# A decoder layer on one core: one row of each q, k, v bias loaded first, and two tiles' projections held back

## The chip, the core and the metric

The kernel runs on one core of a Trainium2 chip. The core has five engines with a queue of instructions each: TensorE (PE, matrix products, with its weight loads shown apart as PEld), VectorE (DVE), ScalarE (ACT), GpSimd (POOL) and SyncE (SP), which issues the copies between the main memory and the core's memory. Every engine works through its queue in order and waits on semaphores for what others make. The time is device microseconds of one execution; smaller is better. The kernel before takes 1658.99 us (median of three runs, 1658.43 to 1659.1).

## The reference

Eight batches of 512 rows by 256 columns pass through three stages, each followed by a residual sum and a normalisation over the columns. All numbers are 32-bit floats. The first stage is the one that the change touches:

```python
xn = layer_norm(x, ln1_w, ln1_b)
q = (xn @ q_w.T + q_b).reshape(B, N, H, D).transpose(0, 2, 1, 3)
k = (xn @ k_w.T + k_b).reshape(B, N, H, D).transpose(0, 2, 1, 3)
v = (xn @ v_w.T + v_b).reshape(B, N, H, D).transpose(0, 2, 1, 3)
q = jax.nn.elu(q) + 1.0
k = jax.nn.elu(k) + 1.0
kv = jnp.einsum('bhnd,bhne->bnde', k, v)
qkv = jnp.einsum('bhnd,bnde->bhne', q, kv)
k_sum = k.sum(axis=1)
qk = jnp.einsum('bhnd,bnd->bhn', q, k_sum)
attn = qkv / qk[..., None]
attn = attn.transpose(0, 2, 1, 3).reshape(B, N, C)
attn = attn @ o_w.T + o_b
x = x + attn
xn2 = layer_norm(x, ln2_w, ln2_b)
h = jax.nn.gelu(xn2 @ fc_w.T + fc_b, approximate=False)
x = x + (h @ proj_w.T + proj_b)
```

The sums over heads (H = 16) are made for each row by itself, so no row needs another row of its batch. The second stage is softmax attention of 16 heads of 64 over a context of 512 rows; here all rows of the context count for every query. The third is an expert network: eight small encoder and decoder pairs are tried on a batch, the one with the least loss is chosen, and its adapter is applied.

## The kernel before, in words

A batch is four tiles of 128 rows, numbered 0 to 3; tile 2 is the third. For each tile the first stage runs as follows (the function `tile_attention`). PE multiplies the normalised, transposed tile `xnT` by the weights `wqkv`: 512 columns of q and k into one PSUM bank, 256 columns of v into another (L512 to L523). The bias is added in one of two ways. For tiles 0 and 1 of the first batch (`EARLY`, L64) PE adds a product of a row of ones with row 0 of `bqkv` (L519); for all others DVE adds the whole of `bqkv`, the same row copied to 128 partitions (L527, L544). ACT makes the exponential part (L531, L532, one buffer `ex`); DVE writes k and q (L554, L566). Then come eight large products over 1088 elements each, on POOL or on DVE, and eight sums on DVE: four for kv (L580, L589) and four for the output (L603, L612; for tiles 0 and 1 of the first batch the latter products are DVE's alone). A reciprocal, a product (L628), a transpose (L653) and a projection (L657) end the tile's attention; a norm and the tile's MLP follow (L737, L712, L717, and the norm L409). In the first batch the cross-attention's first half begins when tiles 0 and 1 are normalised and transposed (L799, then L818); its second half needs tiles 2 and 3.

There are two buffers each for q, k, v and kv, four for products, one for `ex`, one for the transposed tile `xnT`, one for the normalised rows `xhat`, and four PSUM banks beside the two of the attention scores. The next batch's norm takes `xhat` only after the MLP of the first batch's last tile has used it.

The order of the work on each engine is not written by hand. The kernel describes each step as a task with an engine (or a choice of two), an estimated duration, a due time, what it reads and writes, and the weights it needs. A planner (`play`, L161 to L220) then runs a clock: whenever an engine is free it takes, among the tasks that are ready, the one due first, and emits it. The clock is the planner's own; on the chip the engines keep the order but not these times. A task can be ready at the earliest when its weights have arrived by an estimate: `arrive` (L268) counts the bytes of the loads in their order at 185 bytes a nanosecond. A parameter `after` holds a task back until a time on the planner's clock.

`HOLD` (L65) names such times for tiles 2 and 3 of the first batch: their kv products (L596) start at 65000 and 75000 ns at the earliest. Their projections aren't held. Because the projections of tiles 0 and 1 need `wqkv` and `bqkv` by the estimate, and those of tiles 2 and 3 only `wqkv` (L521), the planner puts tile 2's projection ahead of tile 0's.

All loads are issued by SP at the start, in the order of the code: x in four copies, ln1w, ln1b, the three thirds of `wqkv` (L310), the three thirds of `bqkv` (L314, 128 rows of 1 KB, each from the same row in the main memory), woT, bo1 and so on to the context and the next batches' x. SP's queue is not planned by the clock for these. POOL adds bo1 to x for each tile (L376 in the profile, called at L641).

Of the kernel before, what the change touches and what calls it, by code (L numbers as in the profile page):

```python
# [18 lines left out]
P = 128  # L19
B, S, C = 8, 512, 256  # L20
# [41 lines left out]
AFTER = {6: (30, 84)}  # L62

EARLY = (0, 1)  # L64
HOLD = {(0, 2): 65000.0, (0, 3): 75000.0}  # L65


@with_exitstack
def decoder(ctx: ExitStack, tc: tile.TileContext, t: dict, out: bass.AP):
    nc = tc.nc  # L70
# [45 lines left out]
    def task(  # L116
        engine, took, due, emit, reads=(), writes=(), weights=(), kind=None, slack=0.0, holds=(), after=0.0, others=(),
        two=False,
    ):
        k = Task(engine, took, due, emit, kind, slack)  # L120
        k.two = two
        k.on.update((e, (n, wait)) for e, n, wait in others)
        k.at = max([after] + [eta[n] for n in weights])
        before = {}
        for key in reads:
            writers, readers = last.setdefault(key, ([], []))
            before.update((id(d), d) for d in writers)
            readers.append(k)
        for key in writes:
            writers, readers = last.get(key, ([], []))  # L130
            before.update((id(d), d) for d in (*writers, *readers))
            last[key] = ([k], [])
        before.pop(id(k), None)
        for d in before.values():
            d.next.append(k)
        k.unmet = len(before)
        k.vals = list({id(v): v for v in (*(v for v, _ in (*reads, *writes)), *holds)}.values())
        k.makes = [v for v in {id(v): v for v in (*(v for v, _ in writes), *holds)}.values() if v.room]
        for v in k.vals:
            v.left += 1  # L140
        if not k.unmet:
            for e in k.on:
                ready[e].append(k)
        return k
# [123 lines left out]
    def arrive(name, shape):  # L268

        n = 4  # L270
        for s in shape:
            n *= s
        eta["now"] += n / 185
        eta[name] = eta["now"]
# [31 lines left out]
    ln1w, ln1b = column("ln1w", KC), column("ln1b", KC)  # L306
    wqkv = const.tile([P, KC, 3 * C], F32, name="wqkv")
    bqkv = const.tile([P, 3 * C], F32, name="bqkv")
    for i, n in enumerate("qkv"):
        nc.sync.dma_start(  # L310
            out=wqkv[:, :, i * C : (i + 1) * C], in_=t[f"w{n}T"].rearrange("(c p) n -> p c n", p=P)
        )
    for i, n in enumerate("qkv"):
        nc.sync.dma_start(out=bqkv[:, i * C : (i + 1) * C], in_=t[f"b{n}"].partition_broadcast(P))  # L314
    arrive("wqkv", [P, KC, 3 * C])
    arrive("bqkv", [P, 3 * C])
    woT, bo1 = chunked("woT", C, C), row("bo1", C)
# [44 lines left out]
    def mm(cols, n):  # L362

        return n * {512: 858.0, 256: 432.0, 128: 222.0}[cols]
# [102 lines left out]
    def chunks(v, cs=range(NT)):  # L467
        return [(v, (kc, c)) for kc in range(KC) for c in cs]


    def linear_attention(b, begins, step):
# [22 lines left out]
        for c in range(NT):  # L494
            tile_attention(b, c, begins[c], step, x, xnT, y1)
            n2.stats(c, begins[c] + 15.6 * step)
            task(
                "pool", 728, begins[c] + 16 * step,
                lambda e, c=c: add(e, x.t[:, c, :], x.t[:, c, :], y1.t[:, c, :]),
                [(y1, c), (x, c)], [(x, c)], others=[("dve", 420, 4000)], two=True,  # L500
            )
        return y1, n2

    def tile_attention(b, c, due, step, x, xnT, y1):
        cols = slice(c * P, (c + 1) * P)
        qk, ps_v, ex = Val("bank"), Val("bank"), Val("ex")
        q, k, v = Val("q"), Val("k"), Val("v")


        early = b == 0 and c in EARLY  # L510

        def project(ps, lo, hi):  # L512
            for kc in range(KC):
                nc.tensor.matmul(  # L514
                    ps.t[:, : hi - lo], xnT.t[:, kc, cols], wqkv[:, kc, lo:hi], start=kc == 0,
                    stop=kc == KC - 1 and not early,
                )
            if early:
                nc.tensor.matmul(ps.t[:, : hi - lo], ones[0:1, :], bqkv[0:1, lo:hi], start=False, stop=True)  # L519

        needs = ("wqkv", "bqkv") if early else ("wqkv",)  # L521
        task("pe", mm(512, 2 + early), due, lambda: project(qk, 0, 2 * C), chunks(xnT, [c]), [(qk, 0)], needs, "full")
        task("pe", mm(256, 2 + early), due + 1, lambda: project(ps_v, 2 * C, 3 * C), chunks(xnT, [c]), [(ps_v, 0)], needs, "full", holds=[v])  # L523
        if not early:
            task(
                "dve", 690, due + 0.1 * step,
# [44 lines left out]
        kv, o = Val("sc" if early else "kv"), Val("o")  # L571

        def kv_of():
            return kv.t[:, 0, : E1 * D1].rearrange("p (e d) -> p e d", d=D1) if early else kv.t

        for i, s in enumerate(range(0, D1, DSPLIT)):
            pr = Val("prod")

            def kv_product(e, s=s, pr=pr):
                (nc.gpsimd if e == "pool" else nc.vector).tensor_tensor(  # L580
                    pr.t.rearrange("p (d e h) -> p d e h", d=DSPLIT, h=H1),
                    k.t[:, s : s + DSPLIT, :].unsqueeze(2).broadcast_to([P, DSPLIT, E1, H1]),
                    v.t.unsqueeze(1).broadcast_to([P, DSPLIT, E1, H1]),
                    ALU.mult,
                )

            def kv_sum(s=s, pr=pr):

                nc.vector.tensor_reduce(  # L589
                    kv_of()[:, :, s : s + DSPLIT].rearrange("p e d -> p d e"),  # L590
                    pr.t.rearrange("p (d e h) -> p d e h", d=DSPLIT, h=H1),
                    AX.X,
                    ALU.add,
                )

            task("pool", 2490, due + (1 + 1.2 * i) * step, kv_product, [(k, 0), (v, 0)], [(pr, 0)], holds=[kv], after=HOLD.get((b, c), 0.0),  # L596
                 others=[("dve", 1340, 500 if b == 0 else 5000)], two=True)
            task("dve", 1280, due + (2.2 + 1.2 * i) * step, kv_sum, [(pr, 0)], [(kv, s)])
        for i, s in enumerate(range(0, H1, DSPLIT)):
            pr = Val("prod")  # L600
# [623 lines left out]
```

## Time and profile before

| | us |
|---|---|
| median of three runs | 1658.99 |
| the profiled execution, its own time | 1659.94 |
| its span in the profile | 1658.1 |
| PE busy | 1561.0 |
| DVE busy | 1321.9 |
| PE busy in 0 to 40, 40 to 80, 80 to 120 | 22.82, 25.12, 26.50 |
| PE busy in 120 to 160 | 39.91 |
| mean granted clock of PE | 0.978 |

The span is the time from the first to the last instruction that the profile shows; some 1.8 us lie around it. "Busy" is the sum of the times in which an engine had an instruction in work. A line of the timeline gives the start, the duration, the engine, the line of the code, the operation with the tile it writes and the tiles it reads, their shapes and how many instructions are merged; in brackets stands how long the engine had been idle and what released it. A matmul of 32-bit floats is two records. L291 stands for every weight that a small helper loads, and L376 for every plain sum.

### The profile page before, as it was taken

Reading aid. Unit: us, or ns where it says so; the run is one execution under the profiler, and the core shown is the slowest. Engines: PE = TensorE matmul, PEld = TensorE weight load, DVE = VectorE, ACT = ScalarE, POOL = GpSimd, SP = SyncE. Lnnn points to the kernel's source line nnn. Section 1 sums busy time; section 2 is a strip of 40 time slices with the busy share of each in tenths; the row PEclk is TensorE's granted clock in tenths of the full one; section 3 lists DMA queues with packets and bytes.
Section 4 is the critical chain, followed back from the end, with each engine's and each line's share of the span. In section 5 each row is a group of like instructions: output and inputs, shape, how many; then the busy total and the mean of one; then the engine's idle time right before and its main releaser. Section 6 shows DMA issues by size and latency. Waiting matters only on the chain.

```text
span 1658.1 us, 23850 instructions
## 1 busy us (share of the span) xinstructions
PE 1561.0 (94%) x7736; PEld 919.3 (55%) x7736; DVE 1321.9 (80%) x2248; ACT 1055.4 (64%) x2318; POOL 1020.2 (62%) x821
## 2 busy tenths in 40 slices
PE   5579999999999999989999999999999999999995
PEld 3446666654665556645566555555554654654562
DVE  6887996798889898959968899788989756776554
ACT  2257776678656796657765686567666577556543
POOL 6376986786669586758747595656967331443222
PEclk8779999999999999999999999999999999999998
DMA  8000000022112211221122222242222332233300
GB/s 266 1 1 1 1 1 1 7 51 52 51 31 68 67 27 32 57 77 39 38 52 63 79 55 65 60 118 70 66 77 71 95 80 64 74 106 89 90 6 30
DMA packets 176651, 94.43 MB, mean 57 GB/s; under 512 B 19936, under 2 KB 174048, under 8 KB 176528
## 3 DMA queue, kind: packets, MB, share of 16 engines
q1 hardware_dynamic: 175760, 91.32, 20.6%
q0 software_dynamic: 768, 1.60, 0.4%
q8 instruction: 62, 1.02, 0.3%
q14 instruction: 61, 0.50, 0.1%
HBM read 16.30 MB, written 4.19 MB: 12 GB/s over the span
## 4 chain that ended last, share of the span: by engine, by line
PE 64%; DVE 17%; ACT 6%; SPq 5%; issue 4%; POOL 2%; DMA 2%; DVEq 0%; POOLq 0%; ACTq 0%
PE bank L954 10%; PE sc L872 10%; PE bank L970 5%; PE bank L687 5%; SPq L938 5%; PE bank L712 5%; PE bank L918 5%; PE bank L818 4%; DVE nmax L879 4%; PE bank L514 3%; DVE o L612 3%; PE bank L825 2%; ACT p L887 2%; PE bank L992 2%; DVE kv L589 2%
## 5 line engine op out<-in xcount | busy, mean ns | idle before, releaser
L887 ACT ACTIVATE p<-sc,nmax 128x512 f32<-128x512 f32 x512 | 348.5, 691 | 127.5 <-DVE nmax L879 115.8
L898 POOL TENSOR_SCALAR p<-p,rinv 128x512 f32<-128x512 f32 x300 | 209.3, 710 | 294.5 <-DVE rinv L892 275.9
L879 DVE TENSOR_REDUCE nmax<-sc 128x2 f32<-128x1024 f32 x256 | 305.3, 1212 | 69.6 <-PE sc L872 69.3
L580 POOL TENSOR_TENSOR prods<-k,v 128x1088 f32<-128x1088 f32 x115 | 288.9, 2533 | 72.8 <-DVE k L554 38.8
L603 POOL TENSOR_TENSOR prods<-q,kv 128x1088 f32<-128x1088 f32 x107 | 266.7, 2516 | 37.6 <-DVE kv L589 24.8
L872 PE MATMUL sc<-kT,qT 64*128 64x512 f32 x1024 | 267.8, 628 | 4.1 <-ACT kT L371 1.8
L589 DVE TENSOR_REDUCE kv<-prods 128x68 f32<-128x1088 f32 x120 | 152.3, 1272 | 17.8 <-POOL prods L580 17.5
L612 DVE TENSOR_REDUCE o<-prods 128x68 f32<-128x1088 f32 x128 | 161.3, 1270 | 4.6 <-POOL prods L603 4.5
L918 PEld LDWEIGHTS bank<-ident,p 128*128 128x128 f32 x944 | 106.4, 141 | 88.9 <-issue 48.6
L896 ACT ACTIVATE p<-p,rinv 128x512 f32<-128x512 f32 x212 | 143.8, 732 | 6.2 <-DVE rinv L892 6.2
L872 PEld LDWEIGHTS sc<-kT,qT 64*128 64x128 f32 x1024 | 88.1, 188 | 105.4 <-issue 79.2
L908 DVE STREAM_TRANSPOSE blk<-p 128x512 f32<-128x512 f32 x200 | 130.9, 687 | 17.0 <-POOL p L898 9.3
L918 PE MATMUL bank<-ident,p 128*128 128x128 f32 x944 | 134.6, 278 | 9.3 <-ACT qT L829 2.6
L954 PE MATMUL bank<-pT,v 128*64 128x256 f32 x1040 | 128.2, 389 | 5.7 <-DMA pT<-blk 2.7
L954 PE MATMUL bank<-prods,v 128*64 128x256 f32 x1008 | 124.4, 389 | 6.9 <-DMA prods<-prods 6.1
L818 PE MATMUL bank<-x1T,Wq 128*128 128x512 f32 (+1 forms) x288 | 124.7, 556 | 0.8 <-ACT x1T L371 0.5
L970 PE MATMUL bank<-Wo,oT 128*128 128x256 f32 x512 | 121.1, 381 | 0.0
L712 PE MATMUL bank<-projT,h 128*128 128x256 f32 x512 | 119.0, 383 | 1.3 <-ACT kT L371 0.7
L712 PEld LDWEIGHTS bank<-projT,h 128*128 128x128 f32 x512 | 94.9, 190 | 28.1 <-issue 8.3
L970 PEld LDWEIGHTS bank<-Wo,oT 128*128 128x128 f32 x512 | 94.9, 190 | 26.9 <-issue 14.6
L687 PE MATMUL bank<-xT,fcT 128*128 128x512 f32 x224 | 105.9, 600 | 2.2 <-DVE x L717 1.1
L1111 DVE SCALAR_TENSOR_TENSOR h<-bank,decb,xT 128x512 f32<-128x512 f32 x128 | 88.9, 740 | 21.7 <-PE bank L1101 20.7
(140 smaller groups left out, 2676.8 us busy)
## 6 DMA issues: line engine op xcount, KB each, us to landing
prods<-blk SPq DMA_DIRECT2D x480, 64.0 KB, 2.0
pT<-blk SPq DMA_DIRECT2D x320, 64.0 KB, 2.0
prods<-prods SPq DMA_DIRECT2D x176, 64.0 KB, 2.0
pT<-prods SPq DMA_DIRECT2D x128, 64.0 KB, 2.0
x<-in_x SPq DMA_DIRECT2D x7, 512.0 KB, 5.3
out<-x SPq DMA_DIRECT2D x7, 512.0 KB, 3.1
ctx<-in_ctxT SPq DMA_DIRECT2D x8, 256.0 KB, 3.0
fcT<-in_fcT SPq DMA_DIRECT2D x1, 1024.0 KB, 7.7
```

The source lines that it names most:

```text
L580: (nc.gpsimd if e == "pool" else nc.vector).tensor_tensor(pr.t.rearrange("p (d e h) -> p d e h", d=DSPLIT, h=H1), k.t[:, s : s + DSPLIT, : ...
L603: (nc.gpsimd if e == "pool" else nc.vector).tensor_tensor(pr.t.rearrange("p (h e d) -> p h e d", h=DSPLIT, d=D1), q.t[:, s : s + DSPLIT, : ...
L612: nc.vector.tensor_reduce(o.t[:, s : s + DSPLIT, :], pr.t.rearrange("p (h e d) -> p h e d", h=DSPLIT, d=D1), AX.X, ALU.add)
L712: nc.tensor.matmul(ps.t[:, :C], of(f, c), projT[:, f, :], start=f == fs[0], stop=f == fs[-1])
L818: nc.tensor.matmul(ps_q.t[:, :n], Wq[:, kc, cols], x1T.t[:, kc, rows], start=kc == 0, stop=kc == KC - 1)
L872: nc.tensor.matmul(ps.t[:, i, :], qT.t[rows, c * P : (c + 1) * P], kT.t[rows, :], start=True, stop=True)
L879: lambda: nc.vector.tensor_reduce(nmax.t, ps.t, AX.X, ALU.max, negate=True), [(ps, 0)], [(nmax, 0)],
L887: lambda i=i, p=p: nc.scalar.activation(p.t, ps.t[:, i, :], AF.Exp, bias=nmax.t[:, i : i + 1], accum_out=ssum.t[:, i : i + 1]),
L898: nc.gpsimd.tensor_scalar(p.t, p.t, rinv.t[:, i : i + 1], 1.0, ALU.mult, ALU.mult)
L918: nc.tensor.transpose(bank.t[:, m * P : (m + 1) * P], p.t[:, m * P : (m + 1) * P], ident)
L954: nc.tensor.matmul(to, v2.t[:, m, cols], of, start=m == 0, stop=m == NT - 1)
L970: nc.tensor.matmul(ps.t[:, :C], oT.t[:, c * P : (c + 1) * P], Wo[:, pr, :], start=pr == prs[0], stop=pr == prs[-1])
```

## The change

Three edits, all for the first batch. First, each third of the bias is loaded in two copies: row 0 right after the third of the weights that it belongs to, and rows 1 to 127 after all three. Second, in the planner the projections of tiles 0 and 1 no longer need `bqkv`'s estimated arrival, only that of `wqkv`. Third, the time in `HOLD` now holds the two projections of tiles 2 and 3 (both matmul tasks), with 68000 and 78000 ns in place of 65000 and 75000; their products are no longer held by themselves.

```diff
-HOLD = {(0, 2): 65000.0, (0, 3): 75000.0}
+HOLD = {(0, 2): 68000.0, (0, 3): 78000.0}
...
     for i, n in enumerate("qkv"):
         nc.sync.dma_start(
             out=wqkv[:, :, i * C : (i + 1) * C], in_=t[f"w{n}T"].rearrange("(c p) n -> p c n", p=P)
         )
+        nc.sync.dma_start(out=bqkv[0:1, i * C : (i + 1) * C], in_=t[f"b{n}"].partition_broadcast(1))
     for i, n in enumerate("qkv"):
-        nc.sync.dma_start(out=bqkv[:, i * C : (i + 1) * C], in_=t[f"b{n}"].partition_broadcast(P))
+        nc.sync.dma_start(out=bqkv[1:P, i * C : (i + 1) * C], in_=t[f"b{n}"].partition_broadcast(P - 1))
     arrive("wqkv", [P, KC, 3 * C])
     arrive("bqkv", [P, 3 * C])
...
-        needs = ("wqkv", "bqkv") if early else ("wqkv",)
-        task("pe", mm(512, 2 + early), due, lambda: project(qk, 0, 2 * C), chunks(xnT, [c]), [(qk, 0)], needs, "full")
-        task("pe", mm(256, 2 + early), due + 1, lambda: project(ps_v, 2 * C, 3 * C), chunks(xnT, [c]), [(ps_v, 0)], needs, "full", holds=[v])
+        needs, begin = ("wqkv",), HOLD.get((b, c), 0.0)
+        task("pe", mm(512, 2 + early), due, lambda: project(qk, 0, 2 * C), chunks(xnT, [c]), [(qk, 0)], needs, "full", after=begin)
+        task("pe", mm(256, 2 + early), due + 1, lambda: project(ps_v, 2 * C, 3 * C), chunks(xnT, [c]), [(ps_v, 0)], needs, "full", holds=[v], after=begin)
...
-            task("pool", 2490, due + (1 + 1.2 * i) * step, kv_product, [(k, 0), (v, 0)], [(pr, 0)], holds=[kv], after=HOLD.get((b, c), 0.0),
+            task("pool", 2490, due + (1 + 1.2 * i) * step, kv_product, [(k, 0), (v, 0)], [(pr, 0)], holds=[kv],
                  others=[("dve", 1340, 500 if b == 0 else 5000)], two=True)
```

## The prediction

> **What bounds the kernel now.** I read the busy table first, then the busy time by stretches, then the timeline of the first 100 us, then the DMA view of the first 40 us.
>
> ```profile
> PE 1561.0 (94%) x7736; PEld 919.3 (55%) x7736; DVE 1321.9 (80%) x2248; ACT 1055.4 (64%) x2318; POOL 1020.2 (62%) x821
> ...
> 70.00:80.00 10.00, 7.27 (x48) 6.24 (x46) 8.99 (x5) 2.29 (x8) 9.50 (x5) 1.00 0.00 1
> 80.00:90.00 10.00, 1.04 (x3) 0.65 (x4) 9.97 (x13) 0.37 (x1) 8.28 (x4) 0.63 0.00 0
> ...
> 120.00:160.00 40.00, 39.91 (x231) 27.44 (x228) 29.03 (x58) 28.14 (x61) 20.41 (x24) 1.00 0.00 1
> 160.00:200.00 40.00, 37.21 (x225) 25.38 (x223) 38.74 (x55) 28.37 (x65) 36.26 (x19) 1.00 0.01 1
> 200.00:240.00 40.00, 39.77 (x238) 25.75 (x237) 38.27 (x55) 29.15 (x67) 38.66 (x22) 1.00 0.00 1
> ```
>
> The columns after a stretch and its length are PE, PEld, DVE, ACT, POOL, the granted clock and DMA. PE sets the time (94%), but it is full only from about 115 us; in 80 to 90 it works 1.04 us of 10 while DVE works 9.97. In 160 to 240 DVE is full too (77.0 of 80). So a gain or a loss comes from the first 90 us, and DVE has no room to make good after 160.
>
> ```profile
> 10.76 6.36 PE L514 MATMUL bank<-wqkv,xnT 128*128 128x512 f32 x12 [0.47 <-ACT xnT L461]
> ...
> 14.87 2.78 POOL L376 TENSOR_TENSOR y<-x,bo 128x256 f32<-128x256 f32 x4 [7.21 <-DMA bo<-in_bo]
> ...
> 20.56 8.42 POOL L580 TENSOR_TENSOR prods<-k,v 128x1088 f32<-128x1088 f32 x3 [2.91 <-ACT v L536]
> ...
> 30.22 0.58 DVE L554 SCALAR_TENSOR_TENSOR k<-bank,ex 128x256 f32<-128x256 f32 x1
> ...
> 34.26 2.04 PE L834 MATMUL bank<-ctx,Wk 128*128 128x512 f32 x2 [8.05 <-DMA ctx<-in_ctxT]
> ...
> 70.24 7.53 POOL L580 TENSOR_TENSOR prods<-k,v 128x1088 f32<-128x1088 f32 x3
> ...
> 80.04 0.40 DVE L717 TENSOR_TENSOR x<-x,bank 128x256 f32<-128x256 f32 x1
> ...
> 88.49 0.69 PE L799 MATMUL bank<-ident,x 128*128 128x128 f32 x2 [10.63 <-DVE x L409]
> ...
> 89.64 2.07 PE L818 MATMUL bank<-x1T,Wq 128*128 128x256 f32 x4 [0.46 <-ACT x1T L371]
> ```
>
> Each matmul is two records. The first 8 of the 12 at 10.76 are tile 2 (the third), then comes tile 0; the bank, k, q and v that tile 2 fills then lie idle until 70.24. Tile 1's k is written only at 30.22. POOL's adds at 14.87 wait for bo1, and stand in its queue ahead of the products. The cross-attention's first matmul is the one at 89.64; before it PE waits 10.63 us, because tile 1's last steps (L717, the norm, L409) stand in DVE's queue between tile 2's products and sums.
>
> ```profile
> DMA packets 9536, 11.03 MB, mean 276 GB/s; under 512 B 1600, under 2 KB 8256, under 8 KB 9536
> ...
> q1 hardware_dynamic: 9536, 11.03, 88.3%
> ...
> bqkv<-in_bq SPq DMA_DIRECT2D x1, 128.0 KB, 3.8
> ...
> wqkv<-in_wvT SPq DMA_DIRECT2D x1, 256.0 KB, 4.0
> ```
>
> The DMA engines are 88.3% busy in the first 40 us: 0.883 x 16 x 40 / 9536 = 59 ns a packet of 1157 B on average, so some 52 ns for 1 KB.
>
> **The change, part by part.**
>
> *Order at the start.* Tile 0's projection loses tile 2's 8 records ahead of it. PE starts at 10.76 as before, slow at first (weight loads 0.86 apart): 4 x 0.86 + 1.1 for the bias = 15.3; Relu 0.60, Exp 0.63, k 0.59: 17.1. v: 1.1 + 0.6 on PE, copy 0.60: 17.6. Products could start at 17.6, not 20.5: 2.9 earlier. Tile 1's k, q and v get the second buffers at once (about 22, not 30.2).
>
> *The bias copies.* Three 128-row copies become three of one row (1 KB each) and three of 127 rows. SP issues 3 more at 0.45: 1.35 for all that is queued behind them, and 0.47 and 0.9 for wk and wv. Wv issued at 4.52 and landed at 8.5; 9.4 is still ahead of 10.76, so that costs nothing (if PE were ready at once, 0.9). The single rows (nearest: the 1 KB ln1w, 2.3 us) are there long before the bias matmul at 14. No row shows a 127-row copy. One end: it is cut like the 128-row one, and costs what that costs. Other end: one engine takes all of it, since 127 is prime and 16 equal shares cannot be made: 381 packets x 52 ns = 20 us on that engine, against 1.2 on 16, and whatever is queued behind needs that engine too. I take the second end, because every copy on this queue in the trace has a row count that 16 divides and this one has none but 1.
>
> The Trainium skill speaks against this edit: "DMA: Bandwidth & Descriptors", section "Why a DMA increments its semaphore by 16 and not by 1", says that the number of engines must divide the outermost count, and names 127 partitions as a case of one engine. At its 27 GiB/s an engine the 381 KB take, as an estimate, 13.5 us and not 20, and the sum below would be 6.5 less, 1658.
>
> *Who waits for it.* Serial copies start when wv has landed, 8.5, and end at 28.5; woT and bo1 follow, 29.5. On POOL the planner puts bias-bo1 adds ahead of the products: by its arrival sums bo1 comes at 13.3 of its clock (9.1 for wqkv, then 2.1, 1.4, 0.7), tile 0's k is ready at 14.1 (9.1, matmuls 2.6, Relu, Exp and k 1.9, hops 0.5). Two adds of 0.7 come first, so POOL's first product runs at 30.9, 10.3 later than 20.56. DVE makes two of tile 0's four products meanwhile; POOL's other two (2.45 each) end at 35.8, the last sum (1.2) at 37.0, against 30.3. From there DVE owes 8 products and 8 sums (16 x 1.2), 4 sums of tile 1 (4.8) and tile 0's small steps (2): 26, so tile 1's last sum ends at 63, against 56.9. The rest of the weight queue goes 13 to 14 later, so ctx lands at 48, not 34.3; PE's L834 and L825 stand ahead of tile 0's transposes, which move from 46.3 to 54 (cover for this: none, tile 0 is ready at 50).
>
> *Tiles 2 and 3 wait with their projections.* PE's 2.6 us each (4 x 0.43 + 4 x 0.22), DVE's adds 0.70 and 0.60, ACT's 1.23, DVE's k and q 1.0 move behind tile 1's MLP: no instruction is added. Gain: tile 1's tail is free of tile 2. L712 ended at 77.9, L717 began at 80.0 (2.2 late), and from L717's end to L409's end went 8.0, where stats 0.6, 0.15, power 0.55, L409 0.5 and hops 0.3 make 2.1: 8.1 in all. So 63 + (32.7 - 8.1) = 87.6, and tile 0's later MLP in front on PE adds up to 3: cross-attention starts at 88 to 91, where it did. Loss: tile 2's products go from 70.2 to about 92 (its projection 5 us after L712). Of DVE's 19.0 us in 70 to 90, about 5.5 belong to tiles 0 and 1; 13.4 move past the start of the cross-attention. DVE's idle time from there to 160 is 0.7 + 4.0 + 4.2 + 6.8 = 15.6; it stands there for PE and ACT, so I let half be used, 7.8. Left over: 5.6, which nothing takes up in 160 to 240, and for which PE stands. Ends: all absorbed 0, none 13.4.
>
> **Sum.** The profiled run took 1659.94 (span 1658.1 and 1.8 around it), 0.95 above the median of 1658.99. 1659.94 + 5.6 = 1665.5; less 0.95, 1664.6 on the runs' scale: **1665**. All absorbed 1659, none 1672; 3 more where the start slips to 91, 1675.
>
> **Rivals.**
>
> *The copies spread (other side).* Then bo1 lands at 14.87 + 1.35 = 16.2, and POOL's products start at 17.6. Tile 1's last sum: 56.9 - 2.9 - 1.2 (tile 3's adds, gone from DVE's queue) = 52.8. Its transposes no longer wait behind tile 0's MLP (58.3 to 62.7, 4.4): cross-attention at 52.8 + 32.7 - 8.1 - 4.4 = 73 at best. Tile 2's work is then 8 us late instead of 22, so at most the hole of 10.6 counts; DVE's limit after 160 takes some 2: 1659 - 9 = **1650**. For it: the 128-row copy at 3.8 us. Against it: 127. It decides if bo1 lands before 20.5.
>
> *The stall is swallowed.* The copies are serial, but DVE uses all its 15.6 idle us before 160: **1659**. For it: 29.0 of 40 in 120 to 160. Against it: that idle time follows PE and ACT, and tile 3 comes last of the chain that opens batch 1 (one xhat buffer).
>
> *Batch 1 starts late.* Tile 3's MLP gates batch 1's norm; if none of the 13.4 is made good and the start slips too, **1675**. For it: DVE full in 160 to 240.
>
> *The edit does nothing.* If the bias matmul still waited for the 127-row copies, only the hold would act. Under serial copies that adds 13 us of wait at 15 and is worse than the forecast, so it sits in the upper end.
>
> **How the numbers follow.** Forecast 0.44 (its own range 1662.5 to 1670), late batch 1 0.12, swallowed 0.15, spread 0.29. 0.2% (3.3 us) is about what a measurement here can tell from no change. Slower: 0.44 + 0.12 = 0.56; within: 0.15; faster: 0.29. The range goes from the spread case to the late one, 1649 to 1676. A new plan also reorders everything that follows; I put no price on it beyond this range.
>
> **What would show it.** Right: bo1's landing and POOL's first add near 29, POOL's first product near 31, ctx at PE near 48, tile 2's products after 85, PE's wait before L799 shorter than 3, DVE fuller in 120 to 160. Wrong: POOL's adds at 16 (then the first rival); or DVE still at 29 of 40 in 120 to 160 with no loss of PE after 160.

## The result, and the profile after

The changed kernel takes 1668.06 us (median of five runs, 1667.08 to 1672.94); the kernel before, on the same chip, 1658.43 (1656.45 to 1659.10). The ratio is 1.0060, 95% interval 1.0044 to 1.0076: slower by 9.6 us of medians. The profiled execution took 1667.56 us, its span is 1665.8. Line numbers grow by two (L514 is now L516, L580 is L582, L799 is L801, L818 is L820).

The busy table and the busy time by stretches of the kernel after (columns: stretch, length, then PE, PEld, DVE, ACT, POOL, granted clock and DMA):

```profile
PE 1557.0 (93%) x7736; PEld 917.7 (55%) x7736; DVE 1318.5 (79%) x2256; ACT 1052.3 (63%) x2314; POOL 1017.4 (61%) x813
...
70.00:80.00 10.00, 8.52 (x56) 7.40 (x55) 5.49 (x20) 3.09 (x10) 3.53 (x5) 1.00 0.00 0
80.00:90.00 10.00, 8.12 (x34) 5.23 (x35) 3.87 (x10) 2.78 (x4) 1.91 (x3) 1.00 0.00 1
...
120.00:160.00 40.00, 36.15 (x216) 25.88 (x215) 30.88 (x57) 28.58 (x66) 25.30 (x24) 0.96 0.00 1
160.00:200.00 40.00, 37.74 (x211) 25.32 (x210) 36.54 (x47) 23.95 (x55) 32.84 (x15) 1.00 0.00 1
200.00:240.00 40.00, 36.48 (x212) 23.93 (x210) 38.80 (x65) 28.77 (x66) 34.82 (x20) 1.00 0.00 1
```

In 80 to 90 the picture is turned over: PE works 8.12 of 10 (1.04 before) and DVE 3.87 (9.97 before). The hole in front of the cross-attention is gone. The bill comes later: PE loses 3.85, 2.26 and 3.52 us in the last three stretches, 9.6 in all, where it lost 3.1. From 0 to 280 us PE idles 59.8 us in place of 49.1.

The timeline of the kernel after, with the lines that answer to those shown of before, in the same order:

```profile
10.49 3.03 PE L516 MATMUL bank<-wqkv,xnT 128*128 128x512 f32 x4 [0.47 <-ACT xnT L463]
...
27.34 1.40 POOL L378 TENSOR_TENSOR y<-x,bo 128x256 f32<-128x256 f32 x2 [19.95 <-DMA bo<-in_bo]
28.70 8.33 POOL L582 TENSOR_TENSOR prods<-k,v 128x1088 f32<-128x1088 f32 x3
...
21.86 0.58 DVE L556 SCALAR_TENSOR_TENSOR k<-bank,ex 128x256 f32<-128x256 f32 x1
...
46.14 2.04 PE L836 MATMUL bank<-ctx,Wk 128*128 128x512 f32 x2 [25.24 <-DMA ctx<-in_ctxT]
...
89.38 8.40 POOL L582 TENSOR_TENSOR prods<-k,v 128x1088 f32<-128x1088 f32 x3 [2.58 <-DVE k L556]
...
83.06 0.42 DVE L719 TENSOR_TENSOR x<-x,bank 128x256 f32<-128x256 f32 x1 [3.81 <-PE bank L714]
...
85.55 0.44 PE L801 MATMUL bank<-ident,x 128*128 128x128 f32 x2
86.91 1.13 PE L820 MATMUL bank<-x1T,Wq 128*128 128x256 f32 x4 [0.92 <-DVE x1T L375]
```

Tile 0 is first on PE, and tile 1's k is written at 21.86, 8 us earlier than before. But POOL stands 19.95 us for bo1, and its first product comes at 28.70 in place of 20.56, although k and v were ready by 16.9. The context reaches PE at 46.14 in place of 34.26. Tile 1's tail is as short as it can be: from L719's start at 83.06 to the transpose at 85.55 are 2.5 us, where L717's start and L799 were 8.45 apart. Tile 2's first product on POOL comes at 89.38 in place of 70.24.

SyncE's queue of the kernel after shows why bo1 is late, and the DMA view of its first 40 us what the engines did meanwhile (each digit and number is one microsecond). First two issues of the kernel before, then the kernel after:

```profile
6.02 0.43 SPq L314 DMA_DIRECT2D bqkv<-in_bv  x1
6.49 0.43 SPq L291 DMA_DIRECT2D woT<-in_woT  x1
```

```profile
6.04 0.25 SPq L316 DMA_DIRECT2D bqkv<-in_bq  x1
6.33 1.85 SPq L316 DMA_DIRECT2D bqkv<-in_bk  x1
8.22 5.71 SPq L316 DMA_DIRECT2D bqkv<-in_bv  x1
13.97 5.75 SPq L291 DMA_DIRECT2D woT<-in_woT  x1
19.77 0.60 SPq L291 DMA_DIRECT2D bo<-in_bo  x1
```

```profile
DMA  0187388500000000000048459999999999999999
GB/s 0 46 249 230 52 260 280 203 26 23 23 23 23 22 23 23 23 23 22 23 78 301 70 178 400 333 334 359 352 310 294 381 393 426 398 393 364 353 345 366
...
q1 hardware_dynamic: 6410, 8.02, 61.2%
```

From 8 to 20 us the core's DMA engines move 22 to 26 GB/s, against up to 280 just before and mostly over 300 later. The busy share of the queue in the first 40 us falls from 88.3% to 61.2%. In 8 to 20 us the 16 engines together are busy for 0.07 of their time (0.97 before), about one engine's worth: the 127-row copies run at the pace of a single engine, 1 KB in some 45 ns, and the issues behind them (in_bv, woT) take 5.7 us each in place of 0.4.

### The profile page after: what moved, and what is told of

Its sections match the earlier page's. It is cut to its first block, busy times and chain, and to the rows that moved or that the text cites. A ratio compares the mean times of both kernels' runs of the same rounds, so it can differ in the third digit from the quotient of the medians.

```text
span 1665.8 us, 23845 instructions
## 1 busy us (share of the span) xinstructions
PE 1557.0 (93%) x7736; PEld 917.7 (55%) x7736; DVE 1318.5 (79%) x2256; ACT 1052.3 (63%) x2314; POOL 1017.4 (61%) x813
## 4 chain that ended last, share of the span: by engine, by line
PE 61%; DVE 17%; SPq 7%; ACT 6%; issue 4%; DMA 3%; POOL 3%; DVEq 0%; POOLq 0%; ACTq 0%
PE bank L956 10%; PE sc L874 9%; PE bank L714 6%; SPq L940 5%; PE bank L689 5%; PE bank L972 5%; PE bank L920 4%; DVE nmax L881 4%; PE bank L820 3%; PE bank L516 3%; PE bank L827 3%; DVE o L614 3%; PE bank L994 2%; ACT p L889 2%; DVE kv L591 2%
## 5 line engine op out<-in xcount | busy, mean ns | idle before, releaser
L900 POOL TENSOR_SCALAR p<-p,rinv 128x512 f32<-128x512 f32 x291 | 204.3, 714 | 274.0 <-DVE rinv L894 247.6
L582 POOL TENSOR_TENSOR prods<-k,v 128x1088 f32<-128x1088 f32 x113 | 285.1, 2544 | 79.3 <-DVE k L556 42.6
L605 POOL TENSOR_TENSOR prods<-q,kv 128x1088 f32<-128x1088 f32 x110 | 272.5, 2499 | 45.2 <-DVE kv L591 27.0
L898 ACT ACTIVATE p<-p,rinv 128x512 f32<-128x512 f32 x221 | 150.7, 732 | 7.3 <-DVE rinv L894 7.3
L874 PEld LDWEIGHTS sc<-kT,qT 64*128 64x128 f32 x1024 | 86.9, 186 | 102.3 <-issue 73.8
L820 PE MATMUL bank<-x1T,Wq 128*128 128x512 f32 (+1 forms) x288 | 123.7, 552 | 1.5 <-DVE x1T L375 0.9
L972 PEld LDWEIGHTS bank<-Wo,oT 128*128 128x128 f32 x512 | 95.9, 192 | 27.0 <-issue 13.4
```

The lines of the kernel that those rows point to most:

```text
L582: (nc.gpsimd if e == "pool" else nc.vector).tensor_tensor(pr.t.rearrange("p (d e h) -> p d e h", d=DSPLIT, h=H1), k.t[:, s : s + DSPLIT, : ...
L605: (nc.gpsimd if e == "pool" else nc.vector).tensor_tensor(pr.t.rearrange("p (h e d) -> p h e d", h=DSPLIT, d=D1), q.t[:, s : s + DSPLIT, : ...
L874: nc.tensor.matmul(ps.t[:, i, :], qT.t[rows, c * P : (c + 1) * P], kT.t[rows, :], start=True, stop=True)
L900: nc.gpsimd.tensor_scalar(p.t, p.t, rinv.t[:, i : i + 1], 1.0, ALU.mult, ALU.mult)
L972: nc.tensor.matmul(ps.t[:, :C], oT.t[:, c * P : (c + 1) * P], Wo[:, pr, :], start=pr == prs[0], stop=pr == prs[-1])
```

## The experiments

The kernel before ran beside each on the same chip; its medians lay between 1657.1 and 1659.3. So times are compared by the ratio, and "us more" is the ratio less one, times 1658. "Rows" are those of the later copies of the bias, "first product" is tile 2's first on POOL, "MLP 3" is the first matmul of tile 3's MLP, the last step of batch 0 before batch 1 can begin; "PE idle" is 0 to 280 us. "Mark" is a point of the work near 500 us: the start of the 64th of DVE's 256 row maxima of the softmax (L879, at 498.97 in the kernel before), less its time before. "Order" is that of the instructions on DVE, POOL and ACT after this mark: the profiles show two, a and b, which differ nearly to the end of the kernel. These six columns are from the profiled executions, one of each kernel.

| kernel | rows | projections of tiles 2, 3 | cross-attention | first product | MLP 3 | PE idle | mark | order | ratio (95%) | us more |
|---|---|---|---|---|---|---|---|---|---|---|
| before | 128 | free, tile 2 first; products 65, 75 | 89.6 | 70.2 | 140.2 | 49.1 | 0 | a | 1 | 0 |
| after | 127 | held 68, 78 | 86.9 | 89.4 | 150.9 | 59.8 | 9.6 | a | 1.0060 (1.0044 to 1.0076) | 9.9 |
| e1 | 112 | held 68, 78 | 81.4 | 83.9 | 145.4 | 53.0 | 4.8 | a | 1.0049 (1.0035 to 1.0064) | 8.1 |
| e2 | 126 | held 68, 78 | 80.9 | 83.4 | 144.9 | 53.2 | 4.2 | a | 1.0033 (1.0020 to 1.0047) | 5.5 |
| e3 | 127 | as before | 102.1 | 82.7 | 152.4 | 55.4 | 12.2 | a | 1.0069 (1.0054 to 1.0085) | 11.4 |
| e4 | 128 | held 68, 78 | 80.8 | 82.7 | 145.6 | 44.2 | 2.6 | b | 1.0032 (1.0021 to 1.0043) | 5.3 |
| e5 | 127, late | held 68, 78 | 80.7 | 83.1 | 144.6 | 52.7 | 4.0 | a | 1.0048 (1.0035 to 1.0061) | 8.0 |
| e6 | 112 | free; products 65, 75 | 84.5 | 72.4 | 136.0 | 47.2 | -3.4 | a | 0.9997 (0.9987 to 1.0007) | -0.5 |
| e7 | 112 | held 48, 58 | 93.3 | 66.7 | 142.0 | 52.9 | 2.3 | b | 1.0061 (1.0047 to 1.0074) | 10.1 |
| e8 | 112 | held 40, 50 | 91.1 | 69.0 | 139.6 | 56.7 | 7.9 | b | 1.0085 (1.0072 to 1.0098) | 14.1 |
| e9 | 112 | tile 2 free, products 65; tile 3 held 78 | 84.8 | 73.5 | 135.7 | 48.0 | -3.1 | b | 1.0004 (0.9994 to 1.0015) | 0.7 |
| e10 | 112 | free; products 72, 82 | 82.0 | 78.0 | 139.8 | 50.0 | 2.3 | b | 1.0029 (1.0016 to 1.0043) | 4.8 |
| e11 | 128 | free; products 65, 75 | 84.3 | 72.1 | 135.7 | 46.9 | -3.4 | a | 0.9995 (0.9984 to 1.0005) | -0.8 |
| e12 | 112 | free; products 58, 68 | 92.8 | 65.5 | 140.3 | 49.0 | 0.7 | b | 1.0041 (1.0026 to 1.0056) | 6.8 |

PE's idle time of e4 can't be set beside the others: its first matmuls are longer (18.90 us busy for 29 records in 8 to 30; before 16.55 for 40), and PE's busy time is 1571.2 in all, 10 more than before.

The mark shows what a run lost or gained in its first 500 us. Two profiles of kernels with the same order (e6 and e11) agree in it to 0.1 us, while their spans end 5 us apart (1650.4 and 1655.4). From the mark to the end of the span, against the kernel before, the other kernels with order a change by -4.3 to 1.2 us, those with order b by 2.4 to 3.8. So some of what e4, e7 to e10 and e12 lose lies behind 500 us, where the planner put the work in another order; no run took this by itself. The prediction put no price on it; the kernel after has order a, as before, so its own loss holds none of it.

### Which copies are slow

**e1**: the single row becomes 16 rows, the rest 112.

```diff
-  out=bqkv[0:1, ...], in_=t[f"b{n}"].partition_broadcast(1)
+  out=bqkv[0:16, ...], in_=t[f"b{n}"].partition_broadcast(16)
...
-  out=bqkv[1:P, ...], in_=t[f"b{n}"].partition_broadcast(P - 1)
+  out=bqkv[16:P, ...], in_=t[f"b{n}"].partition_broadcast(P - 16)
```

> The changed kernel with its bias copies cut at row 16 in place of row 1: three copies of 16 rows, three of 112; order on all engines as in the changed kernel. Theory (the 127-row copies run on one engine and hold up all that is queued behind them): bo1 reaches POOL near 16 us in place of 27.3, POOL's first product near 17.5 in place of 28.7, ctx reaches PE before 37 in place of 46.1, cross-attention begins at 73 to 79 in place of 86.9, time 1650 (1645 to 1656). Rival (the loss is in the hold of tiles 2 and 3, not in the copies): the start moves, but the time stays over 1663.

**e2**: the rest is cut into 126 rows and one.

```diff
-  out=bqkv[1:P, ...], in_=t[f"b{n}"].partition_broadcast(P - 1)
+  out=bqkv[1 : P - 1, ...], in_=t[f"b{n}"].partition_broadcast(P - 2)
+  out=bqkv[P - 1 : P, ...], in_=t[f"b{n}"].partition_broadcast(1)
```

> The changed kernel with each 127-row copy cut once more: 126 rows and 1 row, so nine small or large copies in all. If what counts is a common divisor with the 16 engines (126 = 14 x 9), bo1 reaches POOL near 17 us and the time is within 4 us of the cut at row 16. If any row count that 16 does not divide is served by one engine, or if copies that begin at row 1 are slow, bo1 still comes near 28 and the time stays at 1664 to 1672.

**e5**: the 127-row copies stay, but SyncE issues them in the course of batch 0.

```diff
-    for i, n in enumerate("qkv"):
-        nc.sync.dma_start(out=bqkv[1:P, ...], in_=t[f"b{n}"].partition_broadcast(P - 1))
...
+        def rest():
+            for i, n in enumerate("qkv"):
+                nc.sync.dma_start(out=bqkv[1:P, ...], in_=t[f"b{n}"].partition_broadcast(P - 1))
+
+        task("sp", 0, 0.0, rest, after=45000.0)
```

> As the kernel after, but the three 127-row copies are issued by SP in the course of the first batch (at 45 us of the planner's clock), behind all the first loads, instead of ahead of woT and bo1. Theory (the copies cost only by what is queued behind them): bo1 at POOL before 16, ctx at PE before 37, cross-attention from 80 to 83, as with copies of 112 rows: 1664 to 1667. Rival (a 127-row copy costs wherever it runs, since it holds SP's queue and one engine): 1668 or more, with later loads (the next batch's x, the weights of stage two) late by some 15.

In all three the order of the work on DVE, ACT and POOL is that of the kernel after. SyncE's queue of e2:

```profile
6.41 0.26 SPq L317 DMA_DIRECT2D bqkv<-in_bq  x1
6.71 0.32 SPq L316 DMA_DIRECT2D bqkv<-in_bk  x1
7.07 0.26 SPq L317 DMA_DIRECT2D bqkv<-in_bk  x1
8.03 0.32 SPq L316 DMA_DIRECT2D bqkv<-in_bv  x1
```

One row fewer in the copy, and the 5.71 us are 0.32: bo1 reaches POOL at 14.0, the context PE at 35.2. So it is the count of 127, as the prediction took it, and neither the number of copies nor that they begin at row 1. In e5 the same slow copies run from 29.9 on (issues of 1.51 and 6.26 us, again mostly 22 to 24 GB/s) and nothing waits for them: the context is at PE at 32.8. A slow copy costs by what is queued behind it.

But all three are still slower than before, by 5.5 to 8.1 us. With the copies mended the cross-attention starts 8 to 9 us earlier than before the change, and the kernel loses more than half of the 9.9 all the same. The prediction's first rival (copies spread: 1650) is refuted, and with it the theory of e1; e1's rival held. The other half of the change costs by itself.

### The copies without the hold, and the hold without the copies

**e3**: before, with only the copies cut into 1 and 127 rows.

```diff
+  out=bqkv[0:1, ...], in_=t[f"b{n}"].partition_broadcast(1)
...
-  out=bqkv[:, ...], in_=t[f"b{n}"].partition_broadcast(P)
+  out=bqkv[1:P, ...], in_=t[f"b{n}"].partition_broadcast(P - 1)
```

> The kernel before, its order on all engines unchanged, with only the bias copies of the change (1 and 127 rows). Theory: bo1 reaches POOL near 27 us, its four adds end at 30, the first product starts near 30 in place of 20.6, ctx comes near 46, cross-attention begins at 95 to 99 in place of 89.6, time 1666 (1662 to 1672). Rival (the copies are hidden behind work that waits anyway): within 3 us of 1658.4.

**e4**: before, with only the hold moved from the products to the projections (128-row copies, and tiles 0 and 1 wait for the bias's estimate as before).

```diff
-HOLD = {(0, 2): 65000.0, (0, 3): 75000.0}
+HOLD = {(0, 2): 68000.0, (0, 3): 78000.0}
...
-  task("pe", mm(512, 2 + early), due, ..., needs, "full")
+  task("pe", mm(512, 2 + early), due, ..., needs, "full", after=HOLD.get((b, c), 0.0))
...
-  kv_product, ..., holds=[kv], after=HOLD.get((b, c), 0.0),
+  kv_product, ..., holds=[kv],
```

The second matmul task, for v, is held in the same way.

> The kernel before with only the hold moved from the products of tiles 2 and 3 to their projections (68000 and 78000 ns), bias copies of 128 rows and the planner's need for the bias as before. Theory: tile 0 comes first on PE all the same, because nothing else is ready; POOL's products begin at 17.5 to 18.5 us, cross-attention at 74 to 80, time 1651 (1646 to 1657). Rival (holding the projections pushes tiles 2 and 3 and so batch 1 back): 1663 or more.

The copies alone cost 11.4 us: the context is at PE at 46.8, tile 2's work stands in tile 1's way as before, the wait of PE for tile 1's norm remains, and the cross-attention starts at 102. PE of e3:

```profile
100.93 0.69 PE L800 MATMUL bank<-ident,x 128*128 128x128 f32 x2 [10.64 <-DVE x L410]
```

The hold alone costs 5.3 (2.6 of it by the mark, the rest in order b), where the theory of e4 had a gain of 7; its rival held. Together they cost 9.9, so the two do not add up. Where the copies are slow, the hold costs nothing that can be told (e3 and after, whose intervals overlap; after has the new order of tile 0 besides, and no run has that order and the slow copies without the hold); where they are fast, it costs 8.6 (e1 less e6, each by its ratio to before on its own chip; e2 in the place of e1 gives 6.0, e5 8.5, and at the mark the three give 7.4 to 8.2). Either half alone loses more than half of the 9.9.

### What in the hold costs

**e6**: fast copies, tiles 0 and 1 first, but the products are held as in the kernel before and the projections are free. Against e1:

```diff
-HOLD = {(0, 2): 68000.0, (0, 3): 78000.0}
+HOLD = {(0, 2): 65000.0, (0, 3): 75000.0}
...
-        needs, begin = ("wqkv",), HOLD.get((b, c), 0.0)
+        needs, begin = ("wqkv",), 0.0
...
-  kv_product, ..., holds=[kv],
+  kv_product, ..., holds=[kv], after=HOLD.get((b, c), 0.0),
```

> Copies of 16 and 112 rows and tiles 0 and 1 first, but no hold on the projections of tiles 2 and 3: their products are held, at 65 and 75 us of the planner's clock, as in the kernel before. Theory (the hold of the projections is what costs in the runs with fast copies): tile 2's products near 70, PE's idle time in 120 to 280 back to 4 to 6 us, 1656 to 1660. Rival (tile 0's earlier start with three products on DVE costs): 1663 to 1667 as with the hold.

Theory held: no difference from before that the measurement can tell. PE's idle time in 120 to 280 is 4.8 us, with the projections held (e1) it was 12.5. Where the 8.6 us come from is seen in the busy time of DVE and POOL ahead of the cross-attention. The stretch 58 to 81 of e1:

```profile
58.00:81.00 23.00, 20.35 (x108) 16.97 (x106) 9.13 (x31) 5.72 (x19) 4.49 (x7) 0.91 0.00 1
```

and of e6:

```profile
58.00:81.00 23.00, 15.35 (x94) 13.04 (x93) 15.35 (x30) 8.50 (x22) 9.48 (x7) 0.95 0.00 0
```

PE does 5 us more there in e1, but DVE (third pair) does 6.2 less and POOL 5.0 less: the kv products and sums of tile 2 are not there yet. They come when the softmax's work wants DVE, and tile 3's MLP is 9.4 us later (145.4 and 136.0). DVE's time alone does not order the runs: in the same stretch it is 11.45 in e9 below, which loses nothing that can be told, and 10.58 in e10, which does. DVE and POOL together order these four: 24.8 in e6, 22.4 in e9, 17.6 in e10 and 13.6 in e1.

**e7 and e8**: e1 with the holds of the projections at 48 and 58, and at 40 and 50.

```diff
-HOLD = {(0, 2): 68000.0, (0, 3): 78000.0}
+HOLD = {(0, 2): 48000.0, (0, 3): 58000.0}
```

> Copies of 16 and 112 rows, projections of tiles 2 and 3 held to 48 and 58 us of the planner's clock in place of 68 and 78. Theory (tiles 2 and 3 start too late, and DVE's idle time before the cross-attention, 14 of 40 us in 40 to 80, goes unused): tile 2's products 15 to 20 us earlier than 84, PE idle in 120 to 280 under 8, 1655 to 1661. Rival (an earlier tile 2 only stands in tile 1's way again, as before the change): the wait of PE for tile 1's norm comes back with 8 to 11 us and the time is 1663 to 1668.

> As the run before, with the holds at 40 and 50. Theory: the earlier the better as long as tile 0's and tile 1's products are through (57 on DVE): 1655 to 1661, within 2 of the hold at 48. Rival: tile 2's projection takes tile 0's and 1's banks and buffers, the cross-attention starts after 90: 1663 to 1669.

My theory "the earlier, the better" fell: 10.1 and 14.1 us more. The old hole is back, as PE's lines before the cross-attention of e7 show:

```profile
75.42 0.38 PE L801 MATMUL bank<-ident,x 128*128 128x128 f32 x2
...
92.10 0.69 PE L801 MATMUL bank<-ident,x 128*128 128x128 f32 x2 [12.79 <-DVE x L411]
```

DVE takes tile 2's sums and products from 70.3 on, ahead of tile 1's last residual and norm.

**e9**: e1 with only tile 3's projection held; the products carry a hold again.

```diff
-HOLD = {(0, 2): 68000.0, (0, 3): 78000.0}
+HOLD = {(0, 2): 65000.0, (0, 3): 78000.0}
...
-        needs, begin = ("wqkv",), HOLD.get((b, c), 0.0)
+        needs, begin = ("wqkv",), HOLD.get((b, c), 0.0) if c == 3 else 0.0
...
-  kv_product, ..., holds=[kv],
+  kv_product, ..., holds=[kv], after=HOLD.get((b, c), 0.0),
```

> Copies of 16 and 112 rows, tile 2 as before the change (projection free, products at 65), only tile 3's projection held (78). Theory (the cost of the hold is that the chain of tile 3, the last before batch 1, runs late, and its projection's work falls where DVE is full): most of the 8 us between the held and the free version is there, 1661 to 1666, and the MLP of tile 3 comes after 141 (136.0 with both free, 145.4 with both held). Rival (it is tile 2's held projection that leaves DVE idle in 60 to 83): 1655 to 1660, tile 3's MLP before 139.

**e10 and e12**: e6 with its products held at 72 and 82, and at 58 and 68.

```diff
-HOLD = {(0, 2): 65000.0, (0, 3): 75000.0}
+HOLD = {(0, 2): 72000.0, (0, 3): 82000.0}
```

> As the version with free projections and fast copies (1656.2), but the products of tiles 2 and 3 are held at 72 and 82 us of the planner's clock in place of 65 and 75. Theory (what has to be early is the projections with their adds, k and q, not the products; tile 1's tail gains if the products stay out of its way): cross-attention from 80 to 85 with PE's wait at L801 under 4, 1652 to 1657. Rival (any delay of tile 2's products moves DVE's work behind the start of the cross-attention and costs what the held projections cost): tile 3's MLP 4 or more later than 136, 1660 to 1666.

> Free projections and fast copies (1656.2 with the products at 65 and 75), products of tiles 2 and 3 held at 58 and 68. So far the later tile 2's first product on POOL, the later the end: 72 gives 1656 to 1658, 78 gives 1662, 84 gives 1666, 89 gives 1668; 66.7 with the projections held at 48 gave 1667. Theory (there is a best start: products before 70 stand in DVE's queue ahead of tile 1's last steps, and the cross-attention starts late): first product 62 to 68, PE's wait at L801 over 9, 1660 to 1667. Rival (the run with the hold at 48 lost because its projection ran beside tile 1's tail, not by its products): 1652 to 1657, PE's wait at L801 no longer than the 7.4 of the version with 65.

Holding tile 3 alone costs nothing that can be told (0.7 us), so the theory of e9 fell: it is tile 2. In e10 the projections are free, only the products wait 5.6 us longer than in e6, and 5.3 us of the 8.6 between e6 and e1 are lost again (5.7 at the mark), with tile 3's MLP 3.8 later; the rival held in time, though the delay came out just under its 4. So what must not be late is tile 2's products and sums. In e1 they are 5.9 us later still, which goes with the other 3.3; that a late projection costs anything beyond this isn't shown. In e12 the products come at 65.5, and tile 1's tail pays, as its theory had it. PE of e12:

```profile
91.65 0.69 PE L801 MATMUL bank<-ident,x 128*128 128x128 f32 x2 [10.85 <-DVE x L411]
```

Among the kernels with fast copies the time is lowest with the first product at 72 to 74 (e6, e9, e11: -0.8 to 0.7 us; the kernel before, at 70.2, has 0) and higher on both sides: 78.0 gives 4.8, 82.7 to 83.9 gives 5.3 to 8.1; 65.5 gives 6.8, 66.7 gives 10.1 and 69.0 (e8) 14.1. So on the early side the first product does not order the runs. All but e1, e2 and e5 of those that lose have order b, but so has e9, which loses nothing that can be told, and at the mark all of them are behind e6, e9 and e11, by 3.8 us and more. The change moved the first product to 89.4.

**e11**: before, with the one word changed that lets tiles 0 and 1 go first.

```diff
-        needs = ("wqkv", "bqkv") if early else ("wqkv",)
+        needs = ("wqkv",)
```

> The kernel before with the one word changed: tiles 0 and 1 need only wqkv's estimated arrival. Copies of 128 rows as before, products held at 65 and 75; the order of PE, DVE, ACT and POOL is that of the version with free projections and fast copies (1656.2). Theory (128-row copies land by 13.9 in any case, PE's bias matmul waits 1 to 2 us at most): within 3 of that version, 1654 to 1660. Rival (the early rows carry its time): PE's bias matmul waits 3 or more for bqkv, tile 0's products after 20, 1660 to 1664.

Theory held: 0.8 us less than before, within the noise, and the same order of work as e6. PE's first lines of e11:

```profile
10.48 3.54 PE L514 MATMUL bank<-wqkv,xnT 128*128 128x512 f32 x4 [0.47 <-ACT xnT L461]
13.94 1.12 PE L519 MATMUL bank<-bqkv,ones 1*128 1x512 f32 x2
```

PE's bias matmul follows with no wait behind the 128-row copies. The early row buys nothing here, and the new order by itself starts the cross-attention 5.4 us earlier, is 3.4 ahead at the mark and ends without a measurable gain. No kernel here beats the kernel before by more than the measurement can tell.

Open is the size on the early side. e12 has PE's idle time of before to 280 us (49.0) and is only 0.7 behind before at the mark, yet it takes 6.8 us more in the median, with a spread of its runs from 1663.1 to 1673.0. Its profile loses 2.8 of its 3.5 us behind the mark, where it has order b; beside e9, which has the same order there, it is 3.8 behind at the mark. In e8 PE loses 9.9 us in 120 to 280, which no run took apart.

## Why the prediction was right, and where it was not

Forecast 1665 against 1668.1: right in sign, 3 us short, within its own range of 1662.5 to 1670. The two costs that it priced are at work, but it was wrong on what each is worth without the other. By its steps:

- **The copies on one engine**: right (e2 against after). Estimated at 52 ns a packet, 20 us in all; the trace gives 22 to 23 GB/s, so 381 KB at 45 ns take 17, of which some 12 stand alone. The Trainium skill ("DMA: Bandwidth & Descriptors", section "Why a DMA increments its semaphore by 16 and not by 1") names 127 partitions as a case of one engine, and the runs agree. The estimate of 13.5 us by the page's 27 GiB/s an engine (section "Specifications") is too low against the 17 us that the measured 45 ns make.
- **Who waits**: DVE's first product was to start at 17.6 (16.9 measured), bo1 was put at 29.5 and POOL's first product at 30.9 (27.3 and 28.7 measured), ctx at 48 (46.1), tile 0's transposes at 54 (52.4), tile 1's last sum at 63 (63.5), the cross-attention at 88 to 91 (86.9), tile 2's products at 92 (89.4). Most came some 2 us earlier than forecast, since the copies did. PE's wait before L799 was to be under 3: none is left.
- **Tiles 2 and 3 late**: the mechanism is right (e1, e6, e10), its term was mis-sized. The prediction pushed 13.4 us of DVE's work past the start of the cross-attention, let 7.8 be absorbed before 160 and left 5.6. Measured, DVE idles 9.6 us in 90 to 160 in place of 15.6, so 6.1 were absorbed; 13.4 less 6.1 is 7.3, and PE idles 8.3 us more in 120 to 280. DVE in 120 to 160 is fuller, as expected, but hardly (30.88, 29.03 before).
- **The step that failed** is in the first rival: "The copies spread ... 1650". With spread copies the runs give 5.5 to 8.1 us more than before, not 9 less. It put tile 1's last sum at 52.8; in e1 it ends at 57.9, no earlier than before (56.9). It put the cross-attention at 73; it starts at 81.4. And it priced the hold at some 2 us where e1 and e6 give 8.6. So that the sign came out right owes something to luck: the forecast made it hang on the slow copies, with 0.29 for a gain without them, while each half of the change alone loses.
- **Swallowed** (1659) and **the edit does nothing** are excluded: PE's bias matmul didn't wait for the 127 rows, tile 0 ran at once. **Batch 1 late** (1675) went halfway: tile 3's MLP came 10.7 us later, and 9.9 were lost. The downstream order that the prediction left unpriced is that of before from some 435 us on, and played no part in the loss.

## What to carry to other kernels

When a hold is moved upstream from a step to the one before it, everything that hangs between the two moves as well; look at which engines then stand idle ahead of the hold and are full behind it (here DVE, in e1: 9.1 of 23 us busy in 58 to 81, then 37.2 of 40 in 80 to 120). Work that fills a gap has a window with two ends: earlier it blocks the chain in front, later it meets the next stage. Here the kernels with fast copies that lose nothing have it between 70.2 and 73.5 us, where the kernel before already had it; those at 69.0 and earlier or at 78.0 and later lose 4.8 us or more. A kernel whose order comes from a planner can also change far behind the edit: compare the order of the work before the times are laid to the edit alone. Before cutting a copy, see that each part still spreads over the DMA engines, and count what stands behind it in the queue.

## What the runs showed of the hardware

A copy on one engine holds up the queue that issued it, too. Behind the 127-row copies SyncE's next issues took 1.85, 5.71 and 5.75 us, so the other engines had nothing to do: 23 GB/s for 12 us. With 126 rows the issues of the copies take 0.26 to 0.33 and woT's 0.39. An issue of that length stands at the end of e2's loads as well (5.63 at 18.14, with all engines busy), so it may be that the queue holds only so much work ahead; that wasn't tried.

DVE and POOL take turns when both make these products. DVE and POOL of e1:

```profile
17.91 4.77 DVE L582 TENSOR_TENSOR prods<-k,v 128x1088 f32<-128x1088 f32 x2 [0.18 <-ACT v L538]
...
17.95 3.58 POOL L582 TENSOR_TENSOR prods<-k,v 128x1088 f32<-128x1088 f32 x1 [1.96 <-ACT v L538]
```

By itself DVE made two such products in 2.49 us (at 16.92 in the kernel after, while POOL waited for bo1), and POOL one in 2.46. In e1, 1.2 for DVE's first, 2.46 for POOL's (ends at 21.5, as recorded) and 1.2 for DVE's second give 22.7, where DVE's two end. The Trainium skill ("SBUF — State Buffer", section "SBUF: two separate sides") calls the port they share an exclusive lock, which fits. It also fits that tile 1's last sum in e1 gained nothing from POOL's start at 18: DVE made three of the eight kv products, where it made one before, and two of the three with POOL in the way (the later one took 3.51).
